# A fused four-layer convolution and attention kernel: compact inversion of the softmax sums through memory, eight single PSUM banks, more added steps per block, and square roots placed ahead of projections

## The chip, the cores and the metric

The kernel runs on one core of one Trainium2 chip. The metric is the device time of one execution in microseconds (us). The engines are called by the names that the profile uses: PE (matmul), PEld (its weight loads), DVE (the vector engine), ACT (the scalar engine), POOL, and SP, which issues DMAs. Each engine runs its own instructions in the order of the program; engines wait for one another through semaphores.

## The reference, cut to what matters

Four layers follow one another on x of shape (16, 384, 16, 16). The change touches the first, an attention over 2 batches of 2048 tokens with 12 heads of 32 channels, whose values are the input itself:

```python
q, k = (qk[0], qk[1])                       # xt @ qk_w.T, per head
v = xt.reshape(B, N, nh, HEAD_DIM).transpose(0, 2, 1, 3)
attn = softmax(einsum('bhnd,bhmd->bhnm', q * scale, k), axis=-1)
attn = alpha * eye + beta * attn - gamma * Cm      # Cm is 1/N everywhere
out = einsum('bhnm,bhmd->bhnd', attn, v)
```

Layer 1 is a 7x7 depthwise convolution, a normalisation over channels, an MLP of 384 to 1536 to 384 with a gelu and a global response norm, and a residual. Layer 2 takes Sobel edges, a 768 to 384 projection, a normalisation and a gelu. Layer 3 has a convolution part, a linear attention, a normalisation and a second MLP of the same size as the first. All arithmetic is in fp32.

## The kernel before, in words

**Two stages.** The first stage is `attention` (line 402). It goes through 6 units (2 batches b by 3 groups g of 128 channels, which are 4 heads). Each unit has 4 blocks n of 512 queries, and each block has 16 steps t of 128 keys: 24 blocks, 384 steps. The second stage is everything after that: layers 1 to 3 for 8 blocks of 512 tokens, `layer1`, `layer2`, `layer3a`, `layer3b` and `layer3c`.

**One attention step.** `scores` (line 467) makes four matmuls, one per head, each 32 rows deep, into two PSUM tiles `st` of two banks each. The pool `pst` has three such tiles (six banks). Two exponentials of 128x1024 on ACT write the SBUF tile `e`. `weighted` (line 485), called one step later, multiplies the four heads of `e` with the values into the one bank `av`, and adds `e` on DVE (128x2048) to a running sum. `ADDS` gives for each block how many steps are added on DVE before the sum goes to PE: with 16 there is one closing sum per block, with 4 there are four. A closing sum is `weights` (line 536), matmuls with ones into the one bank `dn`. All but the last of a block are cut into quarters that later steps take through the dictionary `due`.

**The end of a block.** `va` copies av out and `xg` prepares the residual. `finish` (line 548) copies dn to `r` (all 128 rows hold sums, 32 equal rows per head) and puts further work into `due`: four reciprocals of 128x128 in steps 0 to 3 of the next block, then `scale` (va times r), `put` (the output of the attention), and `check` in step 8, which adds up r for the test whether the fast path was safe. After the last block what is left in `due` is issued at once. In the first step of a block `project` (line 582) makes two projections of q or k for later blocks, each of three matmuls, in one PSUM tile of two banks.

**What fills the gaps.** `fill` (line 1497) is called in every step and places work of the second stage in the attention: the depthwise convolutions of the first two blocks of layer 1 (`conv`), and, from step LEAD = 326 on, the normalisation of these two blocks (`leads`). Work on DVE is started only if `pace` (line 192) leaves time for it in this step. A task that changes from one engine to another rests one or two steps. A square root or gelu is marked `table`, because ACT must load another function table for it.

**The second stage** is ordered by a planner, `plan.all`: it knows a length for each operation, starts the one that can begin first and, within SLACK, the one of the lowest rank (`RANK`). `TURNS` gives the order in which the 16 MLPs (k = 0: layer 1, k = 1: layer 3) run and in which groups they share one load of weights (`wa` for the first matrix, `wb` for the second, three parts of 768 KB each). All instructions of PE, ACT and DVE keep the order in which they are issued by the program; the weight loads go through SP like all other DMAs.

Of the kernel before, what the change touches and what calls it, by code (L numbers as in the profile page):

```python
# [13 lines left out]
PSUM = bass.MemoryType.PSUM  # L14

P = 128
# [20 lines left out]
    (0, ((0, 0), (0, 1), (0, 2), (0, 3),)),  # L37
    (1, ((0, 0), (0, 1), (0, 2),)),
    (0, ((1, 0), (1, 1), (1, 3), (1, 2),)),
    (1, ((0, 3), (1, 0), (1, 3), (1, 1), (1, 2),)),  # L40
# [4 lines left out]
    "mid": ((7.7, 66.1, 2.3, 20.6), (80.0, 9.1, 47.4, 43.4)),  # L45
    "l1": ((104.1, 109.0, 24.6, 77.9), (29.6, 38.6, 11.2, 92.3)),
    "l3c": ((45.9, -4.8, 42.5, 93.4), (141.1, 56.8, 65.9, 24.6)),
    "conv": 118.3,
}
SLACK = 0.134  # L50
JUNK = 2

ADDS = (16, 4, 4, 16, 8, 4, 4, 4, 16, 4, 8, 8, 4, 4, 4, 4, 8, 4, 4, 4, 4, 4, 4, 4)
# [138 lines left out]
def pace(t):  # L192


    n, i = divmod(t - 1, NQC)
    adds = ADDS[n]
    pe, dve = 2.066, 2.2 if t and i % adds else 0.0
    parts = sum(
        min(k + 2 + j * adds // 4, NQC - 1) == i
        for k in range(adds - 1, NQC - 1, adds)  # L200
        for j in range(4)
    )
    pe += 0.22 * parts
    if t and i == NQC - 1 and n < PAIRED:
        pe += 0.87
    elif i == 1 and n > PAIRED:
        pe += 1.67
    elif not parts:
        pe += 0.09
    if n > 0:  # L210
        dve += {0: 0.88, 1: 0.88, 2: 0.88, 3: 0.88, 4: 0.6, 5: 0.66}.get(
            i - 2 * (n > PAIRED), 0.0
        )
    return pe, dve
# [187 lines left out]
def attention(tc, X, xt, L0, block, small, col, cols, ones, load_qk, banks, fill, bound):  # L402
# [6 lines left out]
    with ExitStack() as actx:  # L409
# [6 lines left out]
        pst = pool("pst", 3, space=PSUM)  # L416
        pacc = pool("pacc", 1, space=PSUM)

        def bank2(name):
            return pst.tile([P, 2, BLK], F32, tag="st", name=name)  # L420

        banks.append(lambda name: bank2(name)[:, 0, :])
# [37 lines left out]
        def unit(u, made, gm):  # L460
# [6 lines left out]
            def scores(n, t):  # L467
                es = ep.tile([P, 4, BLK], F32, tag="e", name=f"e_{u}_{n}_{t}")
                sts = [bank2(f"st_{u}_{n}_{t}_{i}") for i in range(2)]
                for h in range(4):  # L470
                    rows = slice(HD * h, HD * (h + 1))
                    pe.matmul(
                        sts[h // 2][:, h % 2, :],
                        keys[t // TB][rows, ts(t % TB, P)],
                        q[n][rows, :],
                        start=True,
                        stop=True,
                    )
                for i in range(2):
                    act.activation(  # L480
                        es[:, 2 * i : 2 * (i + 1), :], sts[i], AF.Exp, scale=HD**-0.5
                    )
                return es

            def weighted(n, t, es):
                if t == 0:
                    acc["av"] = pacc.tile([P, BLK], F32, tag="av", name=f"av_{u}_{n}")
# [48 lines left out]
            def weights(n, t, summed, at):  # L536
                if t == adds[n] - 1 and at.start == 0:
                    acc["dn"] = pacc.tile([P, BLK], F32, tag="dn", name=f"dn_{u}_{n}")
                for h in range(4):
                    pe.matmul(  # L540
                        acc["dn"][HD * h : HD * (h + 1), at],
                        ones[:, :HD],
                        summed[:, h, at],
                        start=(t == adds[n] - 1 and at.start == 0),
                        stop=(t == NQC - 1),
                    )

            def finish(n, va, xg):
# [4 lines left out]
                r = op.tile([P, BLK], F32, tag="r", name=f"r_{u}_{n}")  # L553
                act.activation(r, acc["dn"], AF.Identity, accum_out=bound[:, 0, k : k + 1])

                def invert(i):
                    dve.reciprocal(r[:, ts(i, P)], r[:, ts(i, P)])
# [3 lines left out]

                def check():
                    junk = op.tile([P, BLK], F32, tag="junk", name=f"junk_{u}_{n}", bufs=1)
                    act.activation(junk, r, AF.Identity, accum_out=bound[:, 1, k : k + 1])
# [6 lines left out]
                todo = [*(lambda i=i: invert(i) for i in range(TB)), scale, put]  # L571
                first = (k + 1) * NQC + (0 if k < PAIRED else 2)
                for i, f in [*enumerate(todo), (8, check)]:
                    due.setdefault(first + i, []).append(f)
# [7 lines left out]
        def project(name, steps):  # L582
            pp = bank2(name)
            for copy in [f(pp[:, i, :]) for i, f in enumerate(steps)]:
                copy()
            return 2.7 * len(steps)
# [5 lines left out]
        for u, (b, g) in enumerate(units):  # L592
# [5 lines left out]
            for n in range(NBLK):  # L598
                for t in range(NQC):
# [5 lines left out]
                    if t == 0 and steps:  # L605
                        added = project(f"p_{u}_{n}", steps[:2])
                        del steps[:2]
# [13 lines left out]
def conv_seq_kernel(  # L621
# [869 lines left out]
    if fast:  # L1491
# [5 lines left out]
        def fill(t, added=0.0):  # L1497
# [3 lines left out]
            if t < 0:  # L1501
                while plan.step(bias):
                    pass
                return
            if t % NQC == 9 and t > NQC:
# [4 lines left out]
            for task in (*leads, conv):  # L1510
# [3 lines left out]
                while task is not conv or ("y", 0, YB - 1, NC - 1) not in plan.made:  # L1514
                    op = task.head
                    if before and before.engine != op.engine:
# [152 lines left out]
```

## Time and profile before

| what | value |
|---|---|
| median of three runs | 2682.55 us (2681.45 to 2685.86) |
| the profiled execution | 2685.09 us, its span 2683.3 us |
| attention, first score matmul to last dn matmul | 21.8 to 1053.4 us |
| second stage, from 1053.4 to the end of the span | 1629.9 us |
| PE busy in the span | 2644.4 us (99%) |
| DVE busy | 2007.2 us (75%) |
| ACT busy | 1568.1 us (58%) |
| DMA | 46.18 MB, 5 busy engine-percent |
| table loads on ACT | 96 of 1283 ns |

A group line of the profile says which tile an instruction writes and reads, its shape, how often it occurs, the busy time of the group, the mean length of one instruction in ns, and the idle time of the engine just before, with what ended it. Every fp32 matmul of the program is two matmul instructions in the profile, so the 1536 score matmuls are 3072. A busy PE is not a PE at its peak: matmuls are pipelined, and a waiting PE shows above all in the distance between the starts of equal groups. In the timeline, each line is a run of equal instructions with start and length in us.

### The profile page before, as it was taken

How to read it: one execution, taken by the hardware profiler on the slowest of the kernel's cores; microseconds unless marked ns; L12 is line 12 of the kernel's file. 1: busy time of each engine (PE TensorE's matmuls, PEld its weight loads, DVE VectorE, ACT ScalarE, POOL GpSimd, SP SyncE). 2: the span in 40 equal slices, each digit the busy share in tenths (PEclk: the TensorE clock that was granted, in tenths of full speed). 3: DMA queues.
4: the chain of work that ended last, by engine and by line, in shares of the span. 5: the costliest groups of instructions: out<-in, count | busy, mean ns of one | idle time of the engine just before them, and what ended most of it. 6: DMA issues, size and time to landing. Idle time of an engine off the chain costs nothing. (4 is left out here: it accounts for less than half of the span.)

```text
span 2683.3 us, 31719 instructions
## 1 busy us (share of the span) xinstructions
PE 2644.4 (99%) x12933; PEld 1061.5 (40%) x12933; DVE 2007.2 (75%) x2287; ACT 1568.1 (58%) x2323; POOL 7.5 (0%) x54
## 2 busy tenths in 40 slices
PE   9999999999999999899999999999999999999999
PEld 3332333233333333445444544444444545454443
DVE  5999999999999989899999999996336263532000
ACT  6778788878878887565637532355546344423111
POOL 0000000000000000000000000000000000000000
PEclk9999999999999999999999999999999999999999
DMA  3000000000000003000001000100001000000000
GB/s 149 5 13 1 5 13 5 13 1 5 13 1 1 13 1 109 22 0 1 0 1 36 12 12 24 47 24 24 1 0 36 12 12 12 0 12 0 12 16 21
DMA packets 23275, 46.18 MB, mean 17 GB/s; under 512 B 1488, under 2 KB 10832, under 8 KB 23120
## 3 DMA queue, kind: packets, MB, share of 16 engines
q1 hardware_dynamic: 22976, 43.92, 4.8%
q8 instruction: 103, 1.69, 0.3%
q14 instruction: 52, 0.43, 0.1%
q10 hardware_dynamic: 144, 0.15, 0.0%
HBM read 37.77 MB, written 6.29 MB: 16 GB/s over the span
## 5 line engine op out<-in xcount | busy, mean ns | idle before, releaser
L94 ACT ACTIVATE e<-st 128x1024 f32<-128x1024 f32 x768 | 743.6, 1022 | 108.1 <-PE st L94 91.8
L94 DVE SCALAR_TENSOR_TENSOR y<-l,vec,y 128x420 f32<-128x420 f32 (+8 forms) x1152 | 659.5, 632 | 7.5 <-ACT y L94 1.5
L94 DVE TENSOR_TENSOR s<-s,e 128x2048 f32<-128x2048 f32 x226 | 514.5, 2276 | 16.2 <-ACT e L94 1.4
L94 PE MATMUL st<-q,k 32*128 32x512 f32 x3072 | 472.0, 641 | 2.9 <-ACT e L94 1.9
L94 PE MATMUL av<-e,v 128*32 128x512 f32 x3072 | 410.9, 606 | 0.0
L94 PE MATMUL po_l<-hid_l,wb 128*128 128x512 f32 x576 | 260.0, 602 | 7.6 <-ACT hid_l L94 7.6
L94 PE MATMUL ph_l<-y,wa 128*128 128x512 f32 x576 | 259.3, 594 | 1.0 <-ACT y L94 1.0
L94 PE MATMUL ph_l3c<-d_l3c,wa 128*128 128x512 f32 x576 | 257.3, 594 | 0.0
L94 PE MATMUL po_l3c<-hid_l3c,wb 128*128 128x512 f32 x576 | 254.0, 592 | 0.0
L94 PEld LDWEIGHTS st<-q,k 32*128 32x128 f32 x3072 | 148.8, 183 | 214.0 <-issue 136.6
L94 ACT ACTIVATE hid_l3c<-ph_l3c,vec 128x512 f32<-128x512 f32 x96 | 65.9, 686 | 285.0 <-PE ph_l3c L94 282.8
L94 DVE TENSOR_TENSOR s<-e,e 128x2048 f32<-128x2048 f32 x79 | 180.7, 2287 | 36.7 <-ACT e L94 35.9
L94 DVE SCALAR_TENSOR_TENSOR o_l3c<-po_l3c,vec,l 128x512 f32<-128x512 f32 x24 | 17.5, 748 | 212.6 <-PE po_l3c L94 200.8
L94 PEld LDWEIGHTS av<-e,v 128*32 128x32 f32 x3072 | 60.6, 108 | 292.4 <-issue 274.0
L94 PEld LDWEIGHTS po_l<-hid_l,wb 128*128 128x128 f32 x576 | 110.0, 193 | 141.9 <-issue 124.8
L94 PEld LDWEIGHTS po_l3c<-hid_l3c,wb 128*128 128x128 f32 x576 | 109.3, 190 | 136.1 <-issue 134.4
L94 PEld LDWEIGHTS ph_l<-y,wa 128*128 128x128 f32 x576 | 108.6, 190 | 137.5 <-issue 127.5
L94 PEld LDWEIGHTS ph_l3c<-d_l3c,wa 128*128 128x128 f32 x576 | 108.4, 190 | 137.4 <-issue 130.5
L94 ACT ACTIVATE hid_l<-ph_l,vec 128x512 f32<-128x512 f32 x96 | 65.6, 684 | 137.7 <-PE ph_l L94 137.3
L94 DVE SCALAR_TENSOR_TENSOR g_l3a<-h_l3a,dw,g_l3a 128x450 f32<-128x450 f32 (+1 forms) x192 | 119.2, 693 | 23.9 <-ACT g_l3a L94 23.8
L94 PE MATMUL p<-x,wqk_sb 128*128 128x512 f32 x288 | 132.2, 610 | 1.2 <-DMA x<-in_x_dram 1.2
L94 ACT ACT_TABLE_LOAD x96 | 123.2, 1283 | 8.1 <-PE ph_l L94 3.6
(155 smaller groups left out, 2396.4 us busy)
## 6 DMA issues: line engine op xcount, KB each, us to landing
x<-in_x_dram SPq DMA_DIRECT2D x8, 768.0 KB, 10.4
v<-in_xt_dram SPq DMA_DIRECT2D x24, 256.0 KB, 2.8
out_dram<-o_l3c SPq DMA_DIRECT2D x24, 256.0 KB, 2.0
wa<-in_w_dram SPq DMA_DIRECT2D x6, 768.0 KB, 4.5
wb<-in_w_dram SPq DMA_DIRECT2D x6, 768.0 KB, 7.1
wa<-in_mlp_w_dram SPq DMA_DIRECT2D x6, 768.0 KB, 4.3
wb<-in_mlp_w_dram SPq DMA_DIRECT2D x6, 768.0 KB, 4.5
qkv<-in_qkv_wT_dram SPq DMA_DIRECT2D x3, 576.0 KB, 11.1
```

The lines of the kernel that those rows point to most:

```text
L94: self.last = self.tc.keep_in_program_order(make(*args, **kw))
```

## The change

The edits fall into four parts. First, the softmax sums: since the 32 rows of a head are equal, one row per head is sent to DRAM and read back as 128x16, DVE inverts this compact tile, the result goes to DRAM, and four DMAs read it back, repeated over the 32 rows of each head. All six DMAs are issued by SP. `invert` comes in step 2 of the next block, `check` (now on the compact tile) in step 4, `scale` in step 6 and `put` in step 7. Second, PSUM: one pool of eight single banks replaces the two pools; each head of a step has its own bank and its own exponential of 128x512; av, dn and the projections take banks from the same pool. Third, ADDS has 45 closing sums in place of 79. Fourth, `fill` gets a call ahead of the projections that issues a waiting table operation of the leads, while in all other calls a table operation ends the turn of its task. The last unit makes one projection in its first block and two in its second, where it was two and one. The constants of `pace`, the ranks, SLACK and TURNS are new.

```diff
 TURNS = (
-    (0, ((0, 0), (0, 1), (0, 2), (0, 3),)),
-    (1, ((0, 0), (0, 1), (0, 2),)),
-    (0, ((1, 0), (1, 1), (1, 3), (1, 2),)),
-    (1, ((0, 3), (1, 0), (1, 3), (1, 1), (1, 2),)),
+    (0, ((0, 0), (0, 1), (0, 2),)),
+    (1, ((0, 0),)),
+    (0, ((0, 3),)),
+    (1, ((0, 1),)),
+    (0, ((1, 0), (1, 1),)),
+    (1, ((0, 2),)),
+    (0, ((1, 3),)),
+    (1, ((0, 3),)),
+    (0, ((1, 2),)),
+    (1, ((1, 1), (1, 0), (1, 3), (1, 2),)),
 )
 RANK = {
-    "mid": ((7.7, 66.1, 2.3, 20.6), (80.0, 9.1, 47.4, 43.4)),
...
+    "mid": ((32.4, 40.6, 83.5, 47.6), (47.3, 49.0, 49.8, 34.6)),
...
-SLACK = 0.134
+SLACK = 0.191
-ADDS = (16, 4, 4, 16, 8, 4, 4, 4, 16, 4, 8, 8, 4, 4, 4, 4, 8, 4, 4, 4, 4, 4, 4, 4)
+ADDS = (16, 4, 16, 8, 8, 8, 16, 16, 4, 16, 8, 16, 4, 16, 8, 16, 16, 4, 16, 16, 16, 8, 16, 4)
...
-    pe, dve = 2.066, 2.2 if t and i % adds else 0.0
+    pe, dve = 2.075, 2.2 if t and i % adds else 0.0
...
-    pe += 0.22 * parts
+    pe += 0.21 * parts
+    if i == adds + 1 and parts:
+        pe += 0.15
     if t and i == NQC - 1 and n < PAIRED:
-        pe += 0.87
+        pe += 1.1
     elif i == 1 and n > PAIRED:
         pe += 1.67
-    elif not parts:
+    elif not parts and adds < NQC and i > adds:
         pe += 0.09
     if n > 0:
-        dve += {0: 0.88, 1: 0.88, 2: 0.88, 3: 0.88, 4: 0.6, 5: 0.66}.get(
+        dve += {2: 0.17, 6: 0.6, 7: 0.66}.get(
...
-        pst = pool("pst", 3, space=PSUM)
-        pacc = pool("pacc", 1, space=PSUM)
-        def bank2(name):
-            return pst.tile([P, 2, BLK], F32, tag="st", name=name)
+        pb = pool("pb", 8, space=PSUM, reuse_waits="tile")
+        dp = pool("dp", 2, space=DRAM)
+        def bank(name):
+            return pb.tile([P, BLK], F32, tag="bank", name=name)
...
-                sts = [bank2(f"st_{u}_{n}_{t}_{i}") for i in range(2)]
+                sts = [bank(f"st_{u}_{n}_{t}_{h}") for h in range(4)]
...
-                for i in range(2):
-                    act.activation(
-                        es[:, 2 * i : 2 * (i + 1), :], sts[i], AF.Exp, scale=HD**-0.5
-                    )
+                for h in range(4):
+                    act.activation(es[:, h, :], sts[h], AF.Exp, scale=HD**-0.5)
...
-                r = op.tile([P, BLK], F32, tag="r", name=f"r_{u}_{n}")
-                act.activation(r, acc["dn"], AF.Identity, accum_out=bound[:, 0, k : k + 1])
-                def invert(i):
-                    dve.reciprocal(r[:, ts(i, P)], r[:, ts(i, P)])
+                sums = op.tile([P, BLK], F32, tag="sums", name=f"sums_{u}_{n}", bufs=1)
+                act.activation(sums, acc["dn"], AF.Identity, accum_out=bound[:, 0, k : k + 1])
+                away = dp.tile([4, BLK], F32, tag="away", name=f"away_{u}_{n}")
+                nc.sync.dma_start(away, sums[0:P:HD, :])
+                few = op.tile([P, BLK // HD], F32, tag="few", name=f"few_{u}_{n}")
+                nc.sync.dma_start(few, away.rearrange("h (j k) -> (h j) k", j=HD))
+                r = op.tile([P, BLK], F32, tag="r", name=f"r_{u}_{n}", bufs=1)
+                def invert():
+                    dve.reciprocal(few, few)
+                    back = dp.tile([P, BLK // HD], F32, tag="back", name=f"back_{u}_{n}")
+                    nc.sync.dma_start(back, few)
+                    for h in range(4):
+                        nc.sync.dma_start(
+                            r[ts(h, HD)],
+                            back[ts(h, HD)]
+                            .rearrange("j k -> (j k)")
+                            .unsqueeze(0)
+                            .to_broadcast([HD, BLK]),
+                        )
...
-                todo = [*(lambda i=i: invert(i) for i in range(TB)), scale, put]
-                for i, f in [*enumerate(todo), (8, check)]:
+                for i, f in ((2, invert), (4, check), (6, scale), (7, put)):
                     due.setdefault(first + i, []).append(f)
...
                     if t == 0 and steps:
-                        added = project(f"p_{u}_{n}", steps[:2])
-                        del steps[:2]
+                        fill((u * NBLK + n) * NQC, None)
+                        many = 1 if len(steps) == NBLK - 1 else 2
+                        added = project(f"p_{u}_{n}", steps[:many])
+                        del steps[:many]
...
+            if added is None:
+                for task in leads:
+                    if task.head.table:
+                        plan.step(task)
+                return
...
                     op = task.head
+                    if op.table:
+                        break
```

## The prediction

> **What bounds the kernel now.** I read the page first, then the timeline of TensorE (PE) and of ScalarE (ACT) inside the attention, then the busy times by stage, then the waits and the issues around the hand-over from attention to the second stage. In these lines the fields of a group are: busy time in us, mean ns of one instruction, idle time before.
>
> ```profile
> span 2683.3 us, 31719 instructions
> PE 2644.4 (99%) x12933; PEld 1061.5 (40%) x12933; DVE 2007.2 (75%) x2287; ACT 1568.1 (58%) x2323; POOL 7.5 (0%) x54
> L94 ACT ACTIVATE e<-st 128x1024 f32<-128x1024 f32 x768 | 743.6, 1022 | 108.1 <-PE st L94 91.8
> L94 DVE TENSOR_TENSOR s<-e,e 128x2048 f32<-128x2048 f32 x79 | 180.7, 2287 | 36.7 <-ACT e L94 35.9
> ...
> L94 DVE RECIPROCAL r<-r 128x128 f32<-128x128 f32 x96 | 89.9, 941 | 10.0 <-ACT r L94 9.8
> ...
> 160.71 1.37 PE L94 MATMUL st<-q,k 32*128 32x512 f32 x8
> ...
> 163.01 1.14 PE L94 MATMUL st<-q,k 32*128 32x512 f32 x8
> ...
> 165.08 1.31 PE L94 MATMUL st<-q,k 32*128 32x512 f32 x8
> ...
> 167.32 1.14 PE L94 MATMUL st<-q,k 32*128 32x512 f32 x8
> 159.88 3.94 ACT L94 ACTIVATE e<-st 128x1024 f32<-128x1024 f32 x4 [0.41 <-PE st L94]
> 164.19 4.00 ACT L94 ACTIVATE e<-st 128x1024 f32<-128x1024 f32 x4 [0.36 <-PE st L94]
> 1052.35 0.91 SPq L738 DMA_DIRECT2D wa<-in_w_dram  x2
> 1053.31 2.73 SPq L738 DMA_DIRECT2D wb<-in_w_dram  x3
> 1053.34 13.14 PE L94 MATMUL ph_l<-y,wa 128*128 128x512 f32 x30
> 1054.19 3.39 DVE L94 RECIPROCAL r<-r 128x128 f32<-128x128 f32 x4 [1.91 <-ACT r L94]
> wb<-in_w_dram SPq DMA_DIRECT2D x3, 768.0 KB, 10.5
> 1100.00:1400.00 300.00, 291.94 (x787) 134.20 (x788) 292.72 (x461) 160.46 (x307) 1.69 (x12) 0.98 0.00 1
> 1400.00:1750.00 350.00, 350.00 (x996) 158.82 (x995) 343.00 (x543) 163.81 (x268) 0.84 (x6) 1.00 0.08 25
> ```
>
> The reader is to see five things. PE is the bound almost everywhere. Inside the attention it is not a clean bound: in block 3 (one closing sum, ADDS 16) the starts of the score matmuls stand 2.30, 2.07 and 2.24 us apart, though the same work can go by in 2.07; ACT alternates in the same rhythm between a run of four exponentials and a wait of 0.36 to 0.41. Third, VectorE (DVE) is as full as PE up to about 1750. Fourth, at the hand-over PE goes from the last dn matmul (end 1053.4) straight into ph_l at 1053.34, because the first block was already normalised. Fifth, just there SP issues weight loads that take 10.5 us to land.
>
> From the starts of the score matmuls I take block lengths: 41.8 us with ADDS 16 (blocks 3, 8), 43.0 with 8 (blocks 10, 11, 16), 42.8 with 4 (most). The first step of a block is 8.85 (projections and dn inside). A step without a quarter sum alternates 2.07 and 2.24 to 2.30, one with a quarter sum takes 2.28. Attention runs from 21.8 to 1053.4.
>
> **What the Trainium skill says.** "ScalarE: Activation LUTs", section What ACT_TABLE_LOAD costs: an ACTIVATE with immediate operands takes 186 ns plus 0.833 ns per column and overlaps its neighbour by about 93. For 1024 columns that is 1039 (trace: 1022). "DMA: Bandwidth & Descriptors", section Anatomy of one DMA: about 2 us are fixed, mostly the receipt of the last write; the trace has 2.0 for out and 2.8 for v. Same page, section Queues, rings and completion order: SP's DMAs share one row of rings, consumed in ring order. That agrees with the 10.5 us of wb behind wa.
>
> **The change, part by part.**
>
> *Fewer closing sums.* ADDS gives 79 groups before (x79 in the row above) and 45 after, 34 fewer. DVE gets 34 more additions of 2.2 (start to start), +75, and loses 96 reciprocals of 0.94, -90; the compact one on 128x16 is below 0.2 (rows of 128x3 are 0.15 to 0.17), +4 in all. A group costs PE only the difference of 2.28 to the step that replaces it, so its worth hangs on the next part.
>
> *Single banks.* Two exponentials of 1024 become four of 512. From the page's formula 4 x (186 + 427 - 93) = 2.08 us a step; from the trace, one of 1024 costs about 0.93 in a run of four in 3.81 (505.46), that is 0.08 over its columns, so 4 x 0.505 = 2.02. ACT is now level with PE's 2.07. In return a score matmul waits for one bank, seven banks turn where six did in pairs while no dn is held, and an exponential can start after one head. I expect the alternation to go and take 2.09 per step; ends are 2.07 (PE's floor) and 2.156 (alternation stays). Va, xg, sums and copies add some 3.3 us of ACT per block, beside the 5.2 us of projections.
>
> A block then takes 8.85 + 0.2 + 15 x 2.09 = 40.4 with ADDS 16; 8 adds four quarters of 0.21 and 0.15, 41.4; 4 adds twelve, 43.1. Blocks 0 to 19: 11 x 40.4 + 5 x 41.4 + 4 x 43.1 + 3 for odd first steps = 827, against 858.3 before: -31. Blocks 20 to 23: 37.8 + 41.4 + 35.4 + 42.4 + 2 (leads' matmuls) = 159 against 173.3: -14. Together -46; at 2.07 -53, at 2.156 -23.
>
> *Sums by way of memory.* Inside the attention: sums ready about 9.8 into the block, two hops of 2 to 2.4 land by 14 to 14.7; DVE reaches invert after the third addition, about 16. Back and four broadcasts, 5 us, end at about 21.5; scale comes at 24. Cover 1.5 to 3 us, cost 0; if it is missing, DVE waits at invert, and the next addition and the buffer e behind it. SP's v loads queue behind these waits, but belong to the next unit.
>
> *Square roots.* The leads start at step 326. Their rests put sv at 336 and the root at 337 at the earliest, while the new call looks for a root only at 320 and 336, before the step's own fill; elsewhere a table operation now ends the leads' turn. So no root is issued in the attention: the stall of block 22 (a step of 7.91, counted above) goes, and the first block's root moves behind the attention. Nor is DVE free for it: ADDS 16 in block 20 leaves no time by pace, and attention is 46 shorter with 11 less DVE work, so about 35 us of convolution and normalisation (some 0.62 per tap) fall into the second stage.
>
> *Hand-over.* This is what gives back. The last block's chain: sums 0.85, away 2, few 2, inverse 0.2, back 2, broadcasts 2.4, scale and put 1.45 = 10.9 if the queue is empty. But wa and wb are ready about 1 us before and stand in the same rings; with away behind them (10) it is about 20; with every hop behind loads 33. DVE and ACT are in order, and all of the second stage on DVE stands behind scale and put (5.2 us before). Then the normalisation of block 0, from the rows: sums 1.38, su 1.1, centre 1.75, squares 1.9, sums 1.38, sv 1.1, table 1.28, root 0.69, reciprocal 3.35, product 1.76, affine 0.8, lags 1.5 = 18. PE has nothing else: a gap of 38 (29 to 51), none before.
>
> *Second stage.* It lasted 1630 with 25 of PE gaps, so about 1605 of work, unchanged. TURNS now takes l3c of block 0 after three l1 blocks and goes between the two; ten turns in place of four mean six more sets of six loads of 768 KB (issued some 0.9 us apart at 1053), beside matmuls (three slots; 20 us between the release of a chunk and its next use), cost 0. Mixing helps PE while DVE is late: a convolution costs DVE 90 us for 62 of PE, mid and l3c some 70 for 120. Against that stands the deferred DVE work. I keep 19 to 20 of the 25 gaps, -6 (from -15 to +15).
>
> **Sum.** -46 + 38 - 6 = -14 on the span, 2669; the profiled execution was 2685.1 for a span of 2683.3 and the median is 2682.55, so about the span: forecast 2669.
>
> **Rivals.**
> 1. ACT sets the step. For: 2.08 by the page, and ACT is already busy 4.0 of 4.3. Against: 3.81 for four. At 2.156 attention gives -23, the sum is +9: 2692.
> 2. The hand-over costs more than the attention gives (the slower side). Place: SP's rings at the end of the attention; invert and scale hold DVE, check holds ACT. For: 10.5 us to landing at that very place. Against: SP may issue away before the loads. It decides when PE's gap passes about 52 us; with 33 + 18 and 12 us of convolution still before block 0's normalisation it is 63, and with +2 of late DVE the sum is +19: 2702.
> 3. Hand-over cheap and steps at the floor: -53 + 29 - 15 = -39, 2644. For: DVE idle in the late stage leaves room for a better order. Against: every item must fall well.
> 4. The change does not do what it says for the roots: already my forecast. If they are issued in the attention after all, the gap falls to about 0 and the stall of some 5 comes back: -46 + 5 + 0 - 6 = -47, 2636.
>
> **Chances.** Forecast 0.53, rival 1 0.12, rival 2 0.17, rival 3 0.13, rival 4 0.05. A difference below 0.2% (5.4 us) can't be told from none here. Forecast's own range 2654 to 2682: 0.41 faster, 0.10 within, 0.02 slower. Rivals 3 and 4 are faster (0.18), rival 1 gives 0.04 within and 0.08 slower, rival 2 0.02 within and 0.15 slower. Faster 0.59, within 0.16, slower 0.25. Range 2640 to 2698: it leaves out the ends of rivals 2 and 4.
>
> **What would show it.** Score starts 2.07 to 2.10 apart in blocks of ADDS 16 and no alternation; e rows of 128x512 x1536 at about 600 ns; 45 in s<-e,e; the last dn at about 1007; no table load before it; then a gap on PE of 29 to 51 ended by ACT y, and DVE's reciprocal of few and scale waiting for DMA. Wrong would be: table loads in the attention, steps above 2.15, a gap below 20, or DVE waits at few inside the attention.

## The result, and the profile after

The changed kernel takes 2687.1 us (median; 2684.97 to 2690.2), the kernel before 2685.45 beside it (2681.45 to 2686.66). The ratio is 1.001, with a 95% interval of 1.0004 to 1.0017. That is no difference by the bound of 0.2%. A gain of 14 was forecast. The profiled execution has a span of 2685.1 us, against 2683.3.

In what follows ph_l is the first MLP matmul of layer 1, `y<-l,vec,y` on DVE is a convolution, and su_l and sv_l are the sums of a block's normalisation. First the rows of the page of the changed kernel; its helper line is L101 where it was L94.

```profile
span 2685.1 us, 30687 instructions
...
PE 2621.9 (98%) x11845; PEld 1026.3 (38%) x11845; DVE 2016.1 (75%) x2249; ACT 1603.2 (60%) x3083; POOL 7.5 (0%) x54
...
L101 ACT ACTIVATE e<-st 128x512 f32<-128x512 f32 x1536 | 792.2, 611 | 56.3 <-PE st L101 36.7
L101 DVE TENSOR_TENSOR s<-s,e 128x2048 f32<-128x2048 f32 x294 | 673.6, 2291 | 26.9 <-ACT e L101 3.6
L101 DVE TENSOR_TENSOR s<-e,e 128x2048 f32<-128x2048 f32 x45 | 102.9, 2286 | 35.1 <-ACT e L101 32.1
```

PE is busy for 22.5 us less, and yet the span is no shorter. The closing sums themselves fell by more, from 112.4 to 60.5 us on PE; part of that came back in longer av matmuls (410.9 to 437.2 us), which hide waits. And PE stands still for longer. Its waits in the changed kernel (total, times, longest) say where:

```profile
PE ph_l L101 <- ACT y L101: 20.3, 1, 20.3
PE dn L101 <- DVE s L101: 14.2, 14, 3.6
```

The first is one gap at the hand-over (about 1.0 before). The second is new in size (8.2 before): closing sums that wait for DVE's additions. By place:

| | before | after | difference | forecast |
|---|---|---|---|---|
| last dn ends at | 1053.4 | 1033.6 | -19.8 | -46 |
| PE's gap from there to ph_l | about 0 | 20.35 | +20.4 | +38 |
| from ph_l to the end of the span | 1630.0 | 1631.2 | +1.2 | -6 |
| span | 2683.3 | 2685.1 | +1.8 | -14 |

The attention gave less than half of what was forecast, and the hand-over took all of it back.

**The steps of the attention.** PE in the changed kernel, block 2 (ADDS 16); columns are start, length, engine, operation:

```profile
114.92 1.14 PE L101 MATMUL st<-q,k 32*128 32x512 f32 x8
...
116.98 1.14 PE L101 MATMUL st<-q,k 32*128 32x512 f32 x8
118.06 1.18 PE L101 MATMUL av<-e,v 128*32 128x512 f32 x8
119.17 1.14 PE L101 MATMUL st<-q,k 32*128 32x512 f32 x8
```

ACT in the same stretch:

```profile
116.08 8.38 ACT L101 ACTIVATE e<-st 128x512 f32<-128x512 f32 x16 [0.33 <-PE st L101]
124.64 1.57 ACT L101 ACTIVATE e<-st 128x512 f32<-128x512 f32 x3 [0.18 <-PE st L101]
```

The starts of the scores are 2.06 and 2.19 apart: the alternation is still there, only flatter (it was 2.07 and 2.24 or 2.30). What is stretched now is av (1.18 in place of 1.06). ACT runs sixteen exponentials without a pause, (8.38 - 0.61) / 15 = 0.518 each, 2.07 for four and a small wait on top. Later steps of a block stand 2.14 and 2.11 apart. The mean of a plain step is 2.125, where 2.09 was forecast and 2.155 was before.

**The late blocks.** DVE in the changed kernel towards the end of block 19, then PE at the same place:

```profile
848.92 2.28 DVE L101 TENSOR_TENSOR s<-s,e 128x2048 f32<-128x2048 f32 x1
851.12 0.75 DVE L101 SCALAR_TENSOR_TENSOR l<-va,vec,xg 128x512 f32<-128x512 f32 x1
851.79 19.05 DVE L101 TENSOR_TENSOR s<-s,e 128x2048 f32<-128x2048 f32 x8
870.76 2.29 DVE L101 SCALAR_TENSOR_TENSOR y<-l,vec,y 128x420 f32<-128x420 f32 x4
```

```profile
870.90 1.94 PE L101 MATMUL dn<-s,ones 128*32 128x512 f32 x8 [3.61 <-DVE s L101]
```

After an addition, something that doesn't read its result starts 2.20 later (848.92 to 851.12). Eight additions that each need the one before take 19.05, (19.05 - 2.29) / 7 = 2.39 apart. PE stands still for 3.61 until the last is done.

The kernel before had both distances too. DVE in it, block 19:

```profile
852.10 2.23 DVE L94 TENSOR_TENSOR s<-s,e 128x2048 f32<-128x2048 f32 x1
854.25 0.94 DVE L94 RECIPROCAL r<-r 128x128 f32<-128x128 f32 x1
855.10 2.23 DVE L94 TENSOR_TENSOR s<-s,e 128x2048 f32<-128x2048 f32 x1
...
869.52 4.69 DVE L94 TENSOR_TENSOR s<-s,e 128x2048 f32<-128x2048 f32 x2
```

The reciprocal starts 2.15 after the addition; the pair at 869.52 is 4.69 - 2.29 = 2.40 apart. So with a reciprocal of 0.94 between them two additions stand 3.00 apart, only 0.60 more than without. Counted over the whole traces, 139 additions stand directly behind the one whose result they need in the kernel before, and 230 in the changed kernel: groups are longer, and the reciprocals that stood between additions are gone. All of these are at least 2.38 apart; anything else follows an addition after 2.14 to 2.21 where it does not wait.

**The hand-over.** DVE in the changed kernel after the last dn matmul (which ends at 1033.56):

```profile
1039.64 0.25 DVE L101 RECIPROCAL few<-few 128x16 f32<-128x16 f32 x1 [7.20 <-DMA few<-away]
1046.41 0.69 DVE L101 TENSOR_TENSOR va<-va,r 128x512 f32<-128x512 f32 x1 [6.51 <-DMA r<-back]
1047.20 0.75 DVE L101 SCALAR_TENSOR_TENSOR l<-va,vec,xg 128x512 f32<-128x512 f32 x1
1047.87 3.34 DVE L101 RECIPROCAL s_l<-s_l 128x512 f32<-128x512 f32 x1
1051.25 1.76 DVE L101 TENSOR_TENSOR y<-y,s_l 128x1536 f32<-128x1536 f32 x1
1052.93 7.24 DVE L101 SCALAR_TENSOR_TENSOR y<-l,vec,y 128x416 f32<-128x416 f32 x11
```

ACT and PE there:

```profile
1040.26 1.28 ACT L101 ACT_TABLE_LOAD   x1
1041.55 0.69 ACT L101 ACTIVATE s_l<-sv_l,eps 128x512 f32<-128x512 f32 x1
1053.05 2.22 ACT L101 ACTIVATE y<-y,vec 128x512 f32<-128x512 f32 x3 [10.81 <-DVE y L101]
```

```profile
1053.91 9.69 PE L101 MATMUL ph_l<-y,wa 128*128 128x512 f32 x18 [20.35 <-ACT y L101]
```

The chain reads from top to bottom: the two trips through memory hold DVE for 7.20 and 6.51, put is done at 1047.9, 14.3 after the last dn, and then come the reciprocal, the product and the affine of block 0, 6.0 more. The root itself had been ready since 1042.2, but its reciprocal stands on DVE behind the product with r. Inside the attention no wait of DVE comes from the memory route: of 24 inversions of few and 24 products with r, only the last one of each waits. SP at the hand-over:

```profile
1034.34 0.50 SPq L565 DMA_DIRECT2D away<-sums  x1
1034.95 0.40 SPq L762 DMA_DIRECT2D wa<-in_w_dram  x1
1036.03 0.34 SPq L567 DMA_DIRECT2D few<-away  x1
...
1040.31 0.43 SPq L762 DMA_DIRECT2D wb<-in_w_dram  x1
1042.34 1.73 SPq L575 DMA_DIRECT2D r<-back  x4
```

One weight load goes out between away and few, another between back and r. DVE can use few 3.6 us after its issue; inside the attention the landings that the trace tells are 1.6 to 2.8 after it. That the loads are what slows the trips was not tested.

### The profile page after: what moved, and what is told of

The parts are those of the page before. It is cut to its first block, busy times and chain, and to the rows that moved or that the text cites. A ratio compares the mean times of both kernels' runs of the same rounds, so it can differ in the third digit from the quotient of the medians.

```text
span 2685.1 us, 30687 instructions
## 1 busy us (share of the span) xinstructions
PE 2621.9 (98%) x11845; PEld 1026.3 (38%) x11845; DVE 2016.1 (75%) x2249; ACT 1603.2 (60%) x3083; POOL 7.5 (0%) x54
## 5 line engine op out<-in xcount | busy, mean ns | idle before, releaser
L101 ACT ACTIVATE e<-st 128x512 f32<-128x512 f32 x1536 | 792.2, 611 | 56.3 <-PE st L101 36.7
L101 DVE TENSOR_TENSOR s<-s,e 128x2048 f32<-128x2048 f32 x294 | 673.6, 2291 | 26.9 <-ACT e L101 3.6
L101 DVE SCALAR_TENSOR_TENSOR y<-l,vec,y 128x420 f32<-128x420 f32 (+8 forms) x1152 | 660.6, 633 | 7.6 <-ACT y L101 1.4
L101 PE MATMUL st<-q,k 32*128 32x512 f32 x3072 | 451.2, 642 | 1.6 <-DVE y L101 1.3
L101 PE MATMUL av<-e,v 128*32 128x512 f32 x3072 | 437.2, 606 | 0.0
L101 PE MATMUL ph_l<-y,wa 128*128 128x512 f32 x576 | 260.4, 596 | 20.3 <-ACT y L101 20.3
L101 PE MATMUL po_l<-hid_l,wb 128*128 128x512 f32 x576 | 260.8, 601 | 2.3 <-ACT hid_l L101 2.2
L101 PE MATMUL ph_l3c<-d_l3c,wa 128*128 128x512 f32 x576 | 259.6, 595 | 0.0
L101 PE MATMUL po_l3c<-hid_l3c,wb 128*128 128x512 f32 x576 | 256.3, 593 | 0.0
L101 PEld LDWEIGHTS st<-q,k 32*128 32x128 f32 x3072 | 128.9, 183 | 285.2 <-issue 251.3
L101 PEld LDWEIGHTS av<-e,v 128*32 128x32 f32 x3072 | 79.8, 108 | 300.2 <-issue 274.5
L101 ACT ACTIVATE hid_l3c<-ph_l3c,vec 128x512 f32<-128x512 f32 x96 | 65.8, 686 | 190.2 <-PE ph_l3c L101 189.8
L101 ACT ACTIVATE hid_l<-ph_l,vec 128x512 f32<-128x512 f32 x96 | 65.8, 686 | 175.7 <-PE ph_l L101 175.6
L101 PEld LDWEIGHTS ph_l<-y,wa 128*128 128x128 f32 x576 | 109.6, 191 | 158.1 <-issue 126.8
L101 PEld LDWEIGHTS po_l<-hid_l,wb 128*128 128x128 f32 x576 | 109.2, 192 | 137.1 <-issue 122.9
L101 PEld LDWEIGHTS po_l3c<-hid_l3c,wb 128*128 128x128 f32 x576 | 109.0, 190 | 135.3 <-issue 133.2
L101 PEld LDWEIGHTS ph_l3c<-d_l3c,wa 128*128 128x128 f32 x576 | 108.1, 190 | 136.1 <-issue 129.5
L101 DVE SCALAR_TENSOR_TENSOR o_l3c<-po_l3c,vec,l 128x512 f32<-128x512 f32 x24 | 17.9, 748 | 187.4 <-PE po_l3c L101 186.6
L101 DVE SCALAR_TENSOR_TENSOR g_l3a<-h_l3a,dw,g_l3a 128x450 f32<-128x450 f32 (+1 forms) x192 | 119.2, 694 | 19.8 <-ACT g_l3a L101 19.7
L101 PE MATMUL p<-x,wqk_sb 128*128 128x512 f32 x288 | 131.2, 606 | 1.2 <-DMA x<-in_x_dram 1.2
L101 DVE TENSOR_TENSOR s<-e,e 128x2048 f32<-128x2048 f32 x45 | 102.9, 2286 | 35.1 <-ACT e L101 32.1
```

Of the source, the lines that this page charges most:

```text
L101: self.last = self.tc.keep_in_program_order(make(*args, **kw))
```

## The experiments

Thirteen kernels ran. Each ratio is against the kernel before, run beside it, with its 95% interval. The time of the kernel before itself lies anywhere from 2681.3 to 2686.7, so ratios are compared and not medians. The diffs are against the changed kernel where nothing else is said; dots mark what a cut leaves out. Letters in the expectations name theories; what each says stands in the text with its numbers.

**1. Single banks alone.** The kernel before, with eight single banks and exponentials of 512.

```diff
-                for i in range(2):
-                    act.activation(
-                        es[:, 2 * i : 2 * (i + 1), :], sts[i], AF.Exp, scale=HD**-0.5
-                    )
+                for h in range(4):
+                    act.activation(es[:, h, :], sts[h], AF.Exp, scale=HD**-0.5)
...
```

> The kernel before, with the eight single PSUM banks and the four exponentials of 512 columns alone; sums, ADDS, ranks and TURNS as before. Theory A (ScalarE sets the attention step at about 0.52 us per exponential of 512, so 2.07 to 2.14 per step): a plain step goes from the mean of 2.07 and 2.24 to about 2.12, the last dn matmul ends 0 to 6 us earlier than 1053.4, the total moves by -6 to +4 us. Theory B (the single banks free the step, the extra time in the changed kernel has another cause such as VectorE): plain steps at 2.07 to 2.10 and the last dn at about 1040.

Measured: ratio 1.0019 (1.0011 to 1.0027), last dn at 1056.2, 2.8 later than before, where 0 to 6 earlier was expected: a miss. Plain steps are 2.07 and 2.18 apart, flatter than before, but others are longer: the step in which ACT also adds up r for `check` takes 2.56 where it took 2.44, and blocks 0 to 19 together take 860.6 where they took 858.2. The single banks gain nothing. ACT has about as much to do in a step as PE, and what else it must do in a block then shows; that this is the whole reason is not shown.

**2. Pairs put back.** The changed kernel with two-bank tiles and exponentials of 1024.

> The changed kernel with the three pairs of banks, the two accumulator banks and the exponentials of 1024 columns back; all else as changed. Theory A: ScalarE gets slack again (about 1.9 per step), but plain steps return to 2.07 and 2.24 in turn; attention ends 3 to 10 us later than 1033.6, the total is 0 to +10 us against the changed kernel. Theory B: attention ends 15 us or more later.

Measured: 1.0008 (0.9999 to 1.0016). The last dn ends at 1031.6, 2.0 *earlier* than with single banks; steps are 2.07 and 2.24 again. A miss: an attention later by some us was expected. But 2.0 is no sure gain either: the runs below that leave the steps of the attention as they are (4, 5, 8, 9 and 10) end it anywhere from 1033.1 to 1035.3. The total is the same, because DVE reaches the convolution behind the hand-over at the same time (1052.88 and 1052.93).

**3. Narrow exponentials.** Each exponential covers 448 of 512 columns; an eighth of the exponentials is left out. The tiles e become four fixed ones, filled with ones at the start.

```diff
-                    act.activation(es[:, h, :], sts[h], AF.Exp, scale=HD**-0.5)
+                    act.activation(
+                        es[:, h, :448], sts[h][:, :448], AF.Exp, scale=HD**-0.5
+                    )
...
```

> The changed kernel with each exponential over 448 of its 512 columns (the last eighth of every tile e keeps a constant, so an eighth of the softmax is left out); matmuls, sums and buffers as they are. Theory A: ScalarE falls from about 2.07 to 1.86 per step, PE becomes the bound, plain steps go from the mean 2.125 to 2.07, attention ends 12 to 20 us earlier than 1033.6. Rival (a turn of banks or a PE wait sets the step): plain steps stay at 2.12 and attention ends within 3 us of 1033.6.

Measured: 0.9994 (0.9985 to 1.0003). ACT now pauses in every step (two lines of its timeline, then a line of PE's waits):

```profile
117.78 1.85 ACT L101 ACTIVATE e<-st 128x448 f32<-128x448 f32 x4 [0.21 <-PE st L101]
119.84 1.85 ACT L101 ACTIVATE e<-st 128x448 f32<-128x448 f32 x4 [0.21 <-PE st L101]
```

```profile
PE dn L101 <- DVE s L101: 24.2, 19, 3.9
```

Plain steps stand 2.07 apart throughout, so ACT had made the alternation. But the last dn is only 3.0 earlier, at 1030.6, hardly more than the scatter named under 2, where 12 to 20 were expected: the waits for DVE's sums grow from 14.2 to 24.2. ACT was one brake, DVE seems to be the next one right behind it; 6 and 7 test that.

**4. Root first.** Root, reciprocal and product of block 0 go ahead of the last block's inversion, the affine ahead of check.

```diff
         before()
+        fill(-2)
+        for f in due.pop(min(due)):
+            f()
+        fill(-3)
         while due:
...
```

> The changed kernel with the square root, the reciprocal and the product of block 0 issued behind the last addition and ahead of the last block's invert, scale and put, and the affine ahead of check. Theory C (the gap at the hand-over is the only thing that gives the gain back): the first ph_l matmul starts at 1038 to 1041 in place of 1053.9 and the total falls by 11 to 16 us. Rival D (VectorE sets the second stage up to 1750, so that what PE gains there is lost as a wait later): ph_l starts as early, but the total falls by less than 6 us.

Measured: 1.0168 (1.0151 to 1.0185). PE's gap falls to 7.0 as meant, ph_l starts at 1040.4, and the kernel is 42 us slower than the changed one. The planner orders the second stage from the state at this point, and it found another order (run 5 holds the old one). PE's waits:

```profile
PE pd_l3a L101 <- DVE g_l3a L101: 14.3, 4, 9.7
...
PE pg_l L101 <- DVE gs_l L101: 9.6, 2, 9.2
PE sv_l L101 <- DVE s_l L101: 8.5, 4, 3.6
```

The run says nothing on the gap itself, since two things changed.

**5. Root first, same order.** The same, with the planner told of the old places, so that all of the second stage keeps the changed kernel's order.

> As e4_root_first (root, reciprocal and product of block 0 ahead of the last block's invert, scale and put), but the planner of the second stage is told of these operations at their old places, so that every engine keeps the order of the changed kernel behind them. Theory C (the gap at the hand-over gives the gain back): ph_l starts at 1040 to 1041 as in e4, and the total falls by 11 to 15 us against the changed kernel, to 2672 to 2676. Theory D (VectorE sets the second stage): the total falls by less than 6 us; PE's waits for VectorE behind 1060 grow by what the gap loses.

Measured: 0.9997 (0.999 to 1.0004), 0.13% or 3.5 us below the changed kernel, though ph_l starts 12.7 earlier. DVE in this run:

```profile
1040.88 0.25 DVE L101 RECIPROCAL few<-few 128x16 f32<-128x16 f32 x1 [0.57 <-DMA few<-away]
1047.61 0.69 DVE L101 TENSOR_TENSOR va<-va,r 128x512 f32<-128x512 f32 x1 [6.48 <-DMA r<-back]
1048.34 0.75 DVE L101 SCALAR_TENSOR_TENSOR l<-va,vec,xg 128x512 f32<-128x512 f32 x1
1049.01 7.24 DVE L101 SCALAR_TENSOR_TENSOR y<-l,vec,y 128x416 f32<-128x416 f32 x11
```

PE starts early, and DVE's convolution for the next block, the last line, starts only 3.9 earlier: DVE did the reciprocal in what had been waiting time, but still waits for r from memory. The total follows DVE, not PE. PE after its early start:

```profile
1055.14 4.00 PE L101 MATMUL pb<-sh_L_bn__92,ca 128*128 128x1 f32 x18 [4.32 <-DMA ca<-in_cw1T_dram]
...
1088.11 1.29 PE L101 MATMUL su_l<-s_l,ones 128*128 128x512 f32 x2 [2.72 <-DVE s_l L101]
```

There is a new wait for a weight load, ca, but it is not what counts: at su_l PE still has to wait for DVE. The expected growth of PE's waits for DVE did not come; the time went into the wait for ca and into slower matmuls (the 54 of ph_l between pb and su_l last 26.4 in place of 23.4, at a granted clock of 0.89 in place of 1.00).

**6 and 7. Lighter additions, alone and with the narrow exponentials.** The additions take three of four heads, so a quarter of the softmax sums' work is left out (the fourth head uses another's sums).

```diff
-                    dve.tensor_tensor(acc["sum"], acc["sum"], es, ALU.add)
+                    dve.tensor_tensor(acc["sum"][:, :3, :], acc["sum"][:, :3, :], es[:, :3, :], ALU.add)
...
```

> The changed kernel with VectorE's additions over three of the four heads (the fourth head is divided by another head's sums), so an addition of 1536 columns; ScalarE and PE as they are. Theory E (additions that depend on one another take 2.40 us, not 2.2, so blocks of ADDS 16 hang on VectorE): the waits of dn for s (14.2 us) all but vanish, the last dn ends 10 to 18 us before 1033.6, plain steps stay at a mean of 2.12 (ScalarE). Rival: ScalarE alone sets the attention, the last dn moves by less than 4 us.

> Both: exponentials over 448 of 512 columns and additions over three heads (what e3 and e6 leave out). If ScalarE and VectorE together hold the attention: plain steps at 2.07 and no waits for s, the last dn ends 30 to 42 us before 1033.6. If a third thing holds it: less than the sum of e3 (3 us) and e6.

Measured: 0.9928 (0.9913 to 0.9943) and 0.9811 (0.9796 to 0.9826). The last dn ends at 1013.2 and at 981.8, that is 20.3 and 51.8 earlier. No closing sum waits for DVE in either. With the additions alone the steps still alternate (2.07 and 2.24, or 2.14 and 2.16); with both they are 2.07 throughout and a block is 39.8. 20.3 is more than the 10 to 18 expected, 51.8 more than the 30 to 42. Each brake taken away alone gives 3.0 and 20.3; both together give 51.8, more than twice the sum. In both runs the gap at the hand-over stays at 20 to 21, and all of the gain reaches the end.

**8. The old order.** The changed kernel with TURNS, RANK and SLACK of before.

> The changed kernel with TURNS, RANK and SLACK of the kernel before. If the new order of the second stage is worth something (it takes the later convolutions without a loss): slower than the changed kernel by 5 to 40 us, all of it behind the start of ph_l at 1053.9. If the order is worth nothing: within 5 us.

Measured: 1.0133 (1.0118 to 1.0149), 34 slower than the changed kernel, with the last dn at the same 1033.6. All of the loss lies in the second stage (pd_l3a waits 15.2 for DVE, pg_l 12.1). So the new order is worth 34 in this kernel; the kernel before, with its own order and its own state, takes as long from ph_l on (1630.0 and 1631.2), so the old order was equally good for the old state.

**9. The last block inverted in place.** Only the last block; all others keep the route through memory. The DMAs of this block are left out, and its `check` adds up r.

```diff
...
                 def invert():
+                    if last:
+                        dve.reciprocal(r, sums)
+                        return
                     dve.reciprocal(few, few)
...
```

> The changed kernel, except that the last block's 128x512 sums are inverted on DVE where they are, without memory; all other blocks keep the memory route, and PE's order is unchanged. DVE reached scale 12.9 us after the last dn matmul (7.2 and 6.5 of it waits for DMA); with a reciprocal of 3.34 instead it is 4.2 to 5, so scale, and everything on DVE and PE behind it, comes 7 to 9 us earlier. Theory D (what counts at the hand-over is when DVE can begin its second-stage work): gap on PE 12 to 13.5, ph_l at about 1046, second stage from ph_l still 1631, total 2677 to 2680, ratio 0.997. Theory G (the gap does not matter, because PE's work in the second stage is anyway held elsewhere): gap 12 to 13.5, second stage longer by the same, total 2685, ratio 1.000.

Measured: 0.9981 (0.9973 to 0.9989), 0.29% or 7.8 us below the changed kernel. Theory D's numbers, but for ph_l: it starts at 1048.2, the last dn having ended at 1035.3. DVE:

```profile
1036.05 3.35 DVE L101 RECIPROCAL r<-sums 128x512 f32<-128x512 f32 x1 [1.91 <-ACT sums L101]
1039.44 0.69 DVE L101 TENSOR_TENSOR va<-va,r 128x512 f32<-128x512 f32 x1
...
1047.26 7.24 DVE L101 SCALAR_TENSOR_TENSOR y<-l,vec,y 128x416 f32<-128x416 f32 x11
```

Last dn to convolution is 12.0 in place of 19.4, so 7.4 shorter: the total fell by what DVE's start gained. The compact inversion of 0.25 keeps DVE free where memory's two trips are covered; where they are not, the long one of 3.35 is the shorter way here.

**10. Both hand-over edits (5 and 9).**

> The run before this one, and in addition the root, reciprocal and product of block 0 ahead of the last block's inverse, the order of all else as in the changed kernel. DVE's own start of the convolution moves by 7 to 9 (local inverse) and by the 4 that root-first gained, PE's start by about 13. Theory D: total lower than the changed kernel by 10 to 13, 2673 to 2676, ratio 0.996; ph_l at about 1041 or somewhat earlier and the wait of pb for ca that root-first showed at 4.3 goes. Theory G: no more than 5 below, 2680 or above.

Measured: 0.9978 (0.997 to 0.9987), 8.6 below the changed kernel; 10 to 13 were expected. The convolution starts 10.8 after the last dn, 8.6 sooner than in the changed kernel, so the gain is again DVE's, but the two edits overlap: the reciprocal that 5 put into the waiting time of memory has no such time to hide in any more. PE gets the time back as waiting (su_l for DVE 7.3, where it was 3.2).

**11. The old closing sums.** ADDS of before in the changed kernel.

> The changed kernel with the 79 closing sums of before in place of 45. If dependent additions at 2.40 were the main brake (DVE), 34 fewer additions take 82 us off DVE in the attention while PE gets 34 groups more; waits of dn for s fall from 14.2 to under 5, and plain steps keep the 2.07/2.18 alternation of ACT: attention ends within 5 us of 1033.6. If additions were no brake, the extra closing sums cost PE their full price of about 0.5 to 0.8 each: the attention ends 17 to 27 later, at 1050 to 1060. Placement by the pace model may shift both.

Measured: 1.0379 (1.0363 to 1.0394), the last dn at 1057.6. The waits of dn for s fall to 3.6, as the first alternative says, but the end of the attention is where the second has it. By blocks neither holds: blocks 0 to 19 last 848.8 in place of 841.3, 7.5 for 26 more closing sums, 0.29 each (what PE pays less what DVE is spared), and blocks 20 to 23 last 186 in place of 171. There the normalisation of block 0 now starts earlier (`y<-su_l,y` on DVE at 906, at 1009 in the changed kernel); that the pace model let it in is likely, but was not tested. The rest, some 80 us, lies behind the attention, where the planner meets yet another state. So what a closing sum costs can be read from the first twenty blocks only, and the total is no measure of it.

The same blocks show what the parts of the change were worth in the attention: 858.2 before, 848.8 here, 841.3 in the changed kernel, 841.1 with pairs of banks (run 2). The closing sums give 7.5, the single banks nothing, and all the rest 9.4, in which the sums by way of memory are the largest edit. The forecast had 31 for these blocks.

**12. Both hand-over edits, with pairs of banks.**

> The second run of this call with the pairs of banks and exponentials of 128x1024 back. The pairs alone ended the attention 2.0 us earlier than single banks and gave 2685.8 in total; so 0 to 3 us below the second run, 2671 to 2676, ratio 0.995 to 0.997.

("The second run" is run 10.) Measured: 2676.08 us, 0.9968 (0.9956 to 0.998). It is below both kernels: 0.3% under the one before, 0.4% under the changed one.

**13. Additions that don't depend on each other.** The same number of additions of the same size; every second one writes e instead of the running sum.

```diff
-                    dve.tensor_tensor(acc["sum"], acc["sum"], es, ALU.add)
+                    to = acc["sum"] if at % 2 else es
+                    dve.tensor_tensor(to, to, es, ALU.add)
```

> The changed kernel with the same number of additions of the same shape, but every second one of a group writes the step's own exponentials (e plus e) and not the running sum, so that no addition follows one whose result it reads; half of the exponentials are left out of the softmax sums. Theory B (the term sized wrong was the addition: 2.40 apart where it needs the one before, and I had 2.20): eight in a row stand 2.20 apart again, DVE gets some 0.2 x 250 = 50 us of room in the attention, waits of dn for s fall from 14.2 to under 6, and the last dn comes 8 to 16 us earlier (the run with a quarter of the additions left out gave 20.3 for about 180 us of room), total ratio 0.994 to 0.997. Theory A (the 0.2 lies on DVE beside the exponentials, which set the step): the last dn moves by less than 4 us, as with the narrow exponentials alone (3.0). Theory E (2.40 is the price of 2048 columns and not of the dependence): starts stay 2.40 apart.

Measured: 0.9936 (0.9919 to 0.9952), the last dn at 1013.3, 20.3 earlier, more than expected. DVE at the place shown above:

```profile
846.23 2.28 DVE L101 TENSOR_TENSOR s<-s,e 128x2048 f32<-128x2048 f32 x1
848.43 2.28 DVE L101 TENSOR_TENSOR e<-e 128x2048 f32<-128x2048 f32 x1
850.63 2.28 DVE L101 TENSOR_TENSOR s<-s,e 128x2048 f32<-128x2048 f32 x1
852.84 2.28 DVE L101 TENSOR_TENSOR e<-e 128x2048 f32<-128x2048 f32 x1
```

They are 2.20 apart. The waits of dn for s fall to 4.4, and a block of ADDS 16 without other trouble is 40.4 or 40.8. The first is also the forecast's 40.4, but by luck: its steps are longer than forecast and its first step is 8.46 where 9.05 was forecast. The exponentials are untouched, and plain steps are still 2.07 and 2.19, later 2.12 and 2.13. The edit takes nothing from DVE but the 0.2 between an addition and the next (and adds waits of e for av, 27.6 in all). It ends the attention where run 6 does (1013.2), which took work from DVE in another way.

**What the hand-over experiments say together.** For each kernel: when ph_l starts on PE, when the convolution starts on DVE, the span, and what is left of it after each of the two.

| kernel | PE's gap | ph_l | convolution on DVE | span | after ph_l | after the convolution's start |
|---|---|---|---|---|---|---|
| changed kernel | 20.3 | 1053.9 | 1052.9 | 2685.1 | 1631.2 | 1632.2 |
| root first, same order (5) | 7.0 | 1041.2 | 1049.0 | 2679.8 | 1638.6 | 1630.8 |
| last block in place (9) | 13.0 | 1048.2 | 1047.3 | 2677.9 | 1629.7 | 1630.6 |
| both (10) | 7.0 | 1040.1 | 1043.9 | 2674.3 | 1634.2 | 1630.4 |
| independent additions (13) | 20.2 | 1033.5 | 1032.5 | 2663.4 | 1629.9 | 1630.9 |
| 6 and 3 together (7) | 21.3 | 1003.1 | 1002.2 | 2633.8 | 1630.7 | 1631.6 |

The last column holds within 2 us, over 51 us of the convolution's start; the one before it moves by 9. The traces show where the two engines meet: the next matmul behind ph_l that waits for DVE is su_l. In all six kernels of the table it waits for DVE (2.7 to 7.3 us), and it starts 39.0 to 40.0 after the convolution, while its distance from ph_l goes from 38.0 to 46.9. With one order of the second stage, the end is set by when DVE can begin its part, and PE's gap is a sign of that and not the cost.

## Why the prediction was wrong, point by point

**Additions at 2.2 us: the step that failed.** "DVE gets 34 more additions of 2.2 (start to start), +75" took the distance of an addition to something else for all of them. An addition right behind the one that it needs takes 2.40, so fifteen in a block are 36 of 41 us on DVE, where I had 33. Nor are the 34 all: the change makes 91 more such pairs, so +75 should have been about +92 (an estimate: 91 times 0.19 more). My net change for DVE was -11 (+75 - 90 + 4), and the -90 was too much as well: a reciprocal gone from between two additions saves 0.60, not 0.94. Above all I took the length of a block from PE and ACT alone and never held DVE's pace against it. Run 13 takes the 0.2 away from every pair, the old ones too, and gives 20.3 of the 26 us by which the attention was missed. The number stood in the trace before, in the pair of 4.69. The kernel's own `pace` has the same 2.2, which may be why other work is let in that doesn't fit; that was not tried.

**Steps at 2.09: too low.** "I expect the alternation to go" was wrong. My 0.505 came from an exponential of 1024; measured is 0.518. The Trainium skill, "ScalarE: Activation LUTs", section What ACT_TABLE_LOAD costs, gives 186 + 427 - 93 = 520 ns for 512 columns, and the trace agrees with it; I had both, saw that ACT was level with PE, and still added only 0.02 to PE's 2.07. Four are 2.07, exactly PE's own, and with further work on ACT the two do not run at that pace here: 2.125. That is about the 6 us that run 13 leaves of the miss (an estimate: 0.035 times 15 steps in 11 blocks of ADDS 16). Run 3 shows that ACT made the alternation and that freeing it alone is worth about 3; run 7 that with DVE relieved it is worth another 31 (51.8 less 20.3). Rival 1 had the step at 2.156 and the attention at -23, close to the -19.8, but named only one of the two engines.

**The compact inversion.** Priced "below 0.2", measured 0.25. Inside the attention "cost 0" is right as far as waits go: no inversion and no product waited there, 23 of each. That the 96 long reciprocals are gone from DVE is right too; that they had stood between additions and hidden the 0.2 was overlooked.

**Square roots.** Right. None is issued in the attention: its only table load is the one at its start, and the root of block 0 comes at 1041.6, where the kernel before has two table loads in the attention (at 970.0 and 972.0) and the stall of block 22. That block takes 36.5 us (35.4 was forecast). Blocks 20 and 23 are the ones that missed, 44.1 and 49.1 where 37.8 and 42.4 were forecast; in run 13 they take 39.9 and 45.3, so DVE's additions hold these too.

**Hand-over, 38.** Measured 20.35. The chain was 14.3, between my 10.9 for an empty queue and the 20 with away behind the first loads: SP got away out 0.6 ahead of the first load, and further loads went out between the hops. The normalisation from scratch, 18, was the larger error: sums, centre and squares of block 0 had all been done in the attention, so 6.0 remained. Rival 2 had the right place, and its point of decision, a gap of 52, was far off. But even the right gap is not what it costs. The table above shows that DVE's start sets the end; what it costs is the time for which DVE waits for memory (7.20 and 6.51), and run 9 gets 7.4 of it back.

**Second stage, -6.** Measured +1.2 from ph_l. I expected 35 us of DVE work to fall into it; the stretch from 1060 to 2680 has 17.6 more (1042.9 against 1025.2). The new order suits the new state: with the old one the kernel is 34 longer.

**The sum.** Two errors of opposite sign, +26 in the attention and -18 at the hand-over, with +7 in the second stage, make up the +16 from -14 to +1.8. That the total came as near as it did is luck, for the two errors have nothing to do with each other. The attention could not give 46 with its additions 2.40 apart. DVE's busy share alone would not have told: it is 94% of the attention before, 95% in the changed kernel (956.6 of 1011 us) and 95% in run 13 (938.6 of 991).

## What to carry to other kernels

Price a chain of operations by the distance between two that depend on each other, and count these neighbours: taking something else out from between them makes more of them. Hold every engine that a change loads against the *new* length of the stage, not the old one. Where engines are level, one freed alone can give little, and both together more than the sum (here 3.0 and 20.3, but 51.8). A gap on the bound engine is not its own price: find which engine's start moves the end, by moving one start with the order of everything else held fixed.

## What the runs showed of the hardware that was not expected

An addition of 128x2048 in fp32 is shown as 2.28 or 2.29 us on DVE whether or not the next one depends on it; the Trainium skill, "VectorE: DVE Perf Modes", section The TRN2 errata, gives (2048 + 151) / 0.96 = 2291 ns, and the row's mean of 2291 agrees. The distance to the next one is 2.20 if that one is independent (run 13) and 2.40 if it reads the result. The same page, section The DRAIN you can't avoid, reports for eight copies that a semaphore after each costs nothing extra. Here a link costs 0.20; whether the semaphore or the dependence itself takes it, no run tells apart.

Memory's two small trips (8 KB out and back, 8 KB out again, then four times 64 KB to all rows), with weight loads beside them, took 12.9 us from the last dn matmul to the product, against 4.2 with the reciprocal on chip (run 9).

The order of the second stage is worth tens of us and belongs to one state of the plan: 34 when the order of before meets the new attention, 42 when three operations are moved ahead and the planner is let loose. An experiment at a seam of such a kernel has to hold the order fixed, or it measures the planner.
